# A graph layer's weights in 15 block products, with weight sums made by copies and accumulating transfers

## The chip, the cores and the metric

The kernel runs on one core of one Trainium2 chip. The metric is the device time of one execution in microseconds (us); the kernel before took 729.84 us, the median of three runs (729.0 to 730.84). Engines are named as in the profile: PE is the matrix engine, PEld its weight loads, DVE the vector engine, ACT the scalar engine, POOL the GpSimd engine, SP the engine that issues most transfers. All data are float32. One matrix multiply of the program appears in the profile as two, so 72 multiplies are counted as 144; such a half is called a piece below.

## The reference, cut to what matters

The program is an attention layer over a graph of 384 nodes, then a network of two relational graph layers. Only the second of these two layers is at issue (and the hand-over to it from the first). `l` counts the layers:

```python
x = relu(h_text @ w_in + b_in)                       # 384 x 768
for l in range(2):
    h_in = x
    W = einsum('rb,bio->rio', comp[l], basis[l])     # 4 bases, 6 relations, 768 x 768
    agg = ...                                        # sum over edges, mean per relation and node
    x = relu(agg + x @ root[l] + conv_bias[l]) + h_in
    x = bn_gamma[l] * (x - mean) * rsqrt(var + 1e-5) + bn_beta[l]   # over the nodes
h_final = x @ w_out + b_out
```

The kernel makes the products of x with the four bases and with the root, five products of [384, 768] by [768, 768] in each layer. The edges' part is applied to the four base products as one more matrix product, with a matrix `At` (four times 384 x 384) mixed from the six relations.

## The kernel before

The features lie turned, as `XT` (six chunks of 128 features on the partitions, 384 nodes along the row). A layer runs in this order.

For each base `b` in turn, nodes 0 to 255 and the two halves of features and outputs are taken as a 2 by 2 by 2 block product in seven products, and nodes 128 wide of the third block plainly. The multiplies are recorded at L985 (plain ones) and L979 (those with sums). Each has 384 columns. The weight sums are DVE work (`weight_sums`, L927 and L929; `last_sums`, L935), the feature sums too (`node_sums`, L920). ACT copies results out of PSUM into `H_` (L991 to L1006), and DVE adds others to them (L992, L1000, L1002). Weights come as three transfers a base through the ring of five buffers `wpool`.

Then comes the root, 36 multiplies of 384 columns (L1019) into six PSUM banks. In the first layer the mixes of `At` for that layer follow from L348 on; in the second they are dealt out between the products by the table `between` (L953 to L957): 20 DVE instructions (L348) and four of ACT (L346).

Last come the products of `H_` with `At`, in three pairs of output chunks, each by seven products of six multiplies of 192 columns (L1077). In a pair `p` the program's order is: product `pc` with the first sum; DVE takes it into `XN` (`take`, L1107); DVE normalises the chunk before (`normalise_layer`, L1054 to L1058); product `pa`; `take`; product into `pc` again; `take`; then ReLU on ACT (`rectify`, L1110), adding the old features and the node statistics on DVE with a square root on ACT (`measure`, L1042 to L1049). A bank that is multiplied into again must first have been taken by DVE.

The order on PE, DVE, ACT, POOL and SP is the program's own: each engine works through its instructions as written, and one that waits holds up all that stand behind it on that engine. POOL issues accumulating transfers elsewhere in the kernel: at L852 it adds the second count table in DRAM to `A` in SBUF.

Of the kernel before, what the change touches and what calls it, by code (L numbers as in the profile page):

```python
# [10 lines left out]
F32 = mybir.dt.float32  # L11
# [6 lines left out]
P = 128  # L18
N = 384
# [8 lines left out]
KC = DC // P  # L28
HC = DC // 2
HN = N // 2  # L30
R = 6
# [12 lines left out]


BQ, BK, BV, BIQ, BIK, BIV, B_IN, CB, GAM, BET, NCOL = 0, 8, 16, 24, 32, 40, 48, 54, 66, 78, 90

# [4 lines left out]
def gnn_kernel(ctx: ExitStack, tc: tile.TileContext, out, x, edges, chunks, cols, rows, small,  # L52
               wq, wk, wv, wiq, wik, wiv, wo, w_in, basis, root, w_out):
    nc = tc.nc
# [15 lines left out]
    def next_bank(name, among=range(8)):  # L70

        i = next(i for i in ring if i in among)
        ring.remove(i)
        ring.append(i)
        return bank(i, name)
# [13 lines left out]
    def wload(src, shape, name, whole=False):  # L89
        w = wpool.tile([P, *shape], F32, tag="w", name=name)  # L90
        load_rows(w, src, whole)
        return w
# [279 lines left out]
    with ExitStack() as inner:  # L372
# [358 lines left out]
        for g in range(STEPS + 1):  # L731
            f = g + LEAD
            if g < STEPS:
                turn_probs(g)
            if f < STEPS:
                exponents(f)
            if f - 1 in total:
                normalise(f - 1)
            if f + 1 < STEPS:
                scores(f + 1)  # L740
            if g == STEPS:
                ps_y = next_bank("ps_y", (0,))
                multiply_o(ps_y, 2, 0, range(KD - 1))
            if g > 0:
                gather(g - 1)
            if f + 2 == STEPS:

                w_x = [act_tile("w_x") for _ in range(2)]
                for half in range(2):
                    load_rows(w_x[half], w_in[half])  # L750
                w_first = [wload(basis[0, 0, part], (2, DC), "w_c") for part in range(3)]
                w_first += [wload(basis[0, 1, part], (2, DC), "w_c") for part in range(2)]
        soft_stack.close()
# [152 lines left out]
    with tc.tile_pool(name="conv", bufs=1) as cp:  # L906
# [4 lines left out]
        def block(X, n, i):  # L911

            return X.rearrange("p (c i) n -> p i c n", i=2)[:, i, :, n * P:(n + 1) * P]

        def node_sums(X):
            S = cp.tile([P, 4, 3, P], F32, tag="S", name="S")
            for i, a, b, op in ((0, block(X, 1, 0), block(X, 1, 1), ALU.add), (1, S[:, 0], block(X, 0, 0), ALU.subtract),
                                (2, block(X, 0, 0), block(X, 1, 0), ALU.subtract),
                                (3, block(X, 0, 1), S[:, 1], ALU.subtract)):
                nc.vector.tensor_tensor(S[:, i], a, b, op)  # L920
            return S

        def weight_sums(w):
            T13 = keep.tile([P, 3, 2, HC], F32, tag="hT", name="T13")
            T2 = keep.tile([P, 3, HC], F32, tag="mask8", name="T2")
            for c in range(3):
                nc.vector.tensor_tensor(T13[:, c], w[c][:, :, HC:], w[c][:, 0, :].rearrange("p (o d) -> p o d", o=2),  # L927
                                        ALU.subtract)
                nc.vector.tensor_tensor(T2[:, c], w[c][:, 1, HC:], T13[:, c, 0], ALU.subtract)  # L929
            return T13[:, :, 0], T2, T13[:, :, 1]  # L930

        def last_sums(w, T2):
            T4 = cp.tile([P, 3, HC], F32, tag="T4", name="T4")
            for c in range(3):
                nc.vector.tensor_tensor(T4[:, c], w[c][:, 1, :HC], T2[:, c], ALU.subtract)  # L935
            return T4
# [3 lines left out]
        def load_basis(l, b):  # L940
            w = w_first.pop(0) if w_first else []
            return w + [wload(basis[l, b, part], (2, DC), "w_c") for part in range(len(w), 3)]

# [4 lines left out]
        def mixes(l, r, *bs):  # L948
            return lambda: mix(l, r, At, bs)
# [3 lines left out]
                   (0, 3, 0): shares(4), (0, 3, 1): shares(5),  # L953
                   (0, 3, 4): lambda: [mix(0, r, At) for r in range(1, R)],
                   (1, 0, 0): mixes(1, 0, 0, 1, 2, 3)}
        for i in range(10):
            between[1, (i + 1) // 3, (i + 1) % 3] = mixes(1, 1 + i // 2, *((0, 1), (2, 3))[i % 2])  # L957

# [6 lines left out]
        for l in range(L):  # L965

            H_ = cp.tile([P, B, NT, DC], F32, tag="H", name="H")
            rest = lambda: None
            for b in range(B):
                hs = [[H_[:, b, n, i * HC:(i + 1) * HC] for i in range(2)] for n in range(NT)]  # L970
# [21 lines left out]
                nc.vector.tensor_tensor(hs[0][0], hs[0][0], pb, ALU.add)  # L992
                times(pc, S[:, 0], lambda c: T[0][:, c], True)
                nc.scalar.copy(hs[2][0], pe)
                nc.scalar.copy(hs[2][1], pf)
                nc.scalar.copy(hs[1][1], pc)
                times(pa, S[:, 1], lambda c: T[1][:, c])
                nc.scalar.copy(hs[0][1], pa)
                times(pc, S[:, 3], lambda c: w[c][:, 1, HC:])
                nc.vector.tensor_tensor(hs[0][1], hs[0][1], pc, ALU.add)  # L1000
                times(pa, S[:, 2], lambda c: T[2][:, c])
                nc.vector.tensor_tensor(hs[1][1], hs[1][1], pa, ALU.add)  # L1002
# [10 lines left out]

            w = [wload(root[l, part], (2, DC), "w_c") for part in range(3)]
            XN = xtp.tile([P, KC, N], F32, tag="XT", name="XN")
            pr = [next_bank("ps_c", [i for i in range(8) if i not in kept])[:, :N] for _ in range(KC)]
            for k in range(KC):
                for o in range(KC):
                    nc.tensor.matmul(pr[o], w[k // 2][:, k % 2, o * P:(o + 1) * P], XT[:, k, :], start=(k == 0),  # L1019
                                     stop=(k == KC - 1))  # L1020
                if k == 0:
                    rest()
                go_between(l, B, k)
            room2 = keep.tile([P, KD * N], F32, tag="hT", name="room2")
            spaces = [room2[:, 2304:]]
            if l + 1 < L:
                spaces += [v.rearrange("p i k o -> p (i k o)")[:, i * 768:(i + 1) * 768] for v, n in
                           ((cp.tile([P, 4, 3, P], F32, tag="S", name="sums"), 2),
                            (wpool.tile([P, 2, 6, P], F32, tag="w", name="sums"), 2)) for i in range(n)]
                spaces.append(cp.tile([P, 3, HC], F32, tag="T4", name="sums").rearrange("p c d -> p (c d)")[:, :768])  # L1030
                w = load_basis(l + 1, 0)
            else:

                room = late.tile([P, R * NT * N], F32, tag="A", name="room")
                spaces += [room[:, 3 * D + i * 768:3 * D + (i + 1) * 768] for i in range(5)]
                rowsB = room[:, :3 * D].rearrange("p (j d) -> p j d", j=3)
                for j, r in enumerate((R_BOUT, R_LNG, R_LNB)):
                    nc.scalar.dma_start(rowsB[:, j, :], rows[r:r + 1, :].to_broadcast([P, D]))

            def measure(o):  # L1040
# [38 lines left out]

            T1, T2 = [room2[:, i * 1152:(i + 1) * 1152].rearrange("p (c d) -> p c d", c=6) for i in range(2)]  # L1080
            T4 = keep.tile([P, 6, HN], F32, tag="mask8", name="T4")
            nc.vector.tensor_tensor(T1, q(0, 1), q(0, 0), ALU.subtract)
# [26 lines left out]
            def rectify(o):  # L1109
                nc.scalar.activation(XN[:, o, :], XN[:, o, :], AF.Relu)  # L1110
                return o
# [6 lines left out]
            pa = first_of(0)  # L1118
            for p in range(pairs):
                times(pr[2 * p][:, :HN], h(2 * p, 1), q(1, 0))  # L1120
            for o in range(KC):
                begin(o)
            take(0, 0, pa)
            ready = None
            for p in range(pairs):
                last = p == pairs - 1
                sums = iter(()) if last else feature_sums(p + 1)
                o0, o1 = 2 * p, 2 * p + 1
# [34 lines left out]
            XT = XN  # L1163
            if l + 1 < L:
                S = node_sums(XT)
                T = weight_sums(w)


        for t in range(NT):
            nc.gpsimd.tensor_tensor(x_sb[:, t, :], x_sb[:, t, :], rowsB[:, 2, :], ALU.add)  # L1170
        w = [wload(w_out[part], (2, D), "w_out") for part in range(3)]
        hf_ = cp.tile([P, NT, D], F32, tag="H", name="hf")
# [97 lines left out]
```

## Time and profile before

| What | Value |
|---|---|
| median of the runs | 729.84 us |
| the profiled execution's own time | 717.47 us |
| its span, first to last instruction | 715.7 us |
| first layer: last pair's products with `At` | 516.72 to 526.6 us |
| second layer: bases and root | 527.7 to 636.3 us |
| second layer: products with `At` | 636.3 to 677.3 us |
| last matrix product and layer norm | 677.3 to 715.7 us |

The profile numbers instructions by engine, line and shape. A group line gives how often it ran, the us in which it kept its engine busy and the mean ns of one. Matrix pieces overlap: one of 384 columns is listed at 486 ns, yet the next starts about 322 ns later; what counts for time is the distance between starts. A chain line gives a start, a length and what ran. A timeline line is alike, with the idle time before it in brackets.

### The profile page before, as it was taken

Reading aid. Unit: us, or ns where it says so; the run is one execution under the profiler, and the core shown is the slowest. Engines: PE = TensorE matmul, PEld = TensorE weight load, DVE = VectorE, ACT = ScalarE, POOL = GpSimd, SP = SyncE. Lnnn points to the kernel's source line nnn. Section 1 sums busy time; section 2 is a strip of 40 time slices with the busy share of each in tenths; the row PEclk is TensorE's granted clock in tenths of the full one; section 3 lists DMA queues with packets and bytes.
Section 4 is the critical chain, followed back from the end, with each engine's and each line's share of the span. In section 5 each row is a group of like instructions: output and inputs, shape, how many; then the busy total and the mean of one; then the engine's idle time right before and its main releaser. Section 6 shows DMA issues by size and latency. Waiting matters only on the chain.

```text
span 715.7 us, 9149 instructions
## 1 busy us (share of the span) xinstructions
PE 699.9 (98%) x3228; PEld 527.9 (74%) x3228; DVE 512.6 (72%) x1307; ACT 157.6 (22%) x360; POOL 308.1 (43%) x239
## 2 busy tenths in 40 slices
PE   8999999999999999999999999999999999999995
PEld 7759999999997444478985555558975555579943
DVE  5886697868886699787534279798878766507756
ACT  3211111111111577410221124202131111011100
POOL 1366777778687788687786542000000000120000
PEclk9999999999999999999999999999999999999999
DMA  8788787373562622733424994311104322700001
GB/s 303 267 279 264 228 250 212 80 243 67 203 209 43 177 2 1 221 44 45 89 0 103 250 288 153 133 44 45 45 0 133 102 69 94 308 1 1 1 30 59
DMA packets 69180, 91.04 MB, mean 127 GB/s; under 512 B 22940, under 2 KB 50688, under 8 KB 68750
## 3 DMA queue, kind: packets, MB, share of 16 engines
q1 hardware_dynamic: 46830, 78.45, 32.6%
q0 software_dynamic: 21296, 9.60, 10.8%
q10 hardware_dynamic: 1008, 2.41, 0.9%
q8 instruction: 25, 0.41, 0.2%
q14 instruction: 21, 0.17, 0.1%
HBM read 79.27 MB, written 11.16 MB: 126 GB/s over the span
## 4 chain that ended last, share of the span: by engine, by line
PE 87%; DVE 10%; ACT 2%; DMA 1%; issue 0%; DVEq 0%; ACTq 0%
PE ps_g L985 12%; PE ps_g L979 10%; PE ps_k L402 10%; PE ps_c L1077 10%; PE ps_v L402 8%; PE ps_q L420 6%; PE ps_q L402 5%; PE ps_f L1183 4%; DVE At L348 4%; PE ps_y L402 3%; PE ps_c L1019 3%; PE ps_x L402 3%; PE ps_o L707 2%; PE ps_s L662 2%; PE ps_pT L696 2%; PE ps_v L586 2%
## 5 line engine op out<-in xcount | busy, mean ns | idle before, releaser
L283 POOL DMA_INDIRECT atab<-count,at x99 | 166.3, 1679 | 44.2 <-issue 23.5
L278 POOL DMA_INDIRECT mtab<-m_val,at x99 | 103.4, 1045 | 57.6 <-issue 22.9
L1170 POOL TENSOR_TENSOR x_sb<-x_sb,room 128x1024 f32<-128x1024 f32 x3 | 7.0, 2348 | 188.9 <-DMA room<-in_rows 188.9
L348 DVE SCALAR_TENSOR_TENSOR At<-A,small_sb,At 128x1152 f32<-128x1152 f32 x40 | 53.6, 1414 | 0.0
L979 PE MATMUL ps_g<-T,S 128*128 128x384 f32 x144 | 49.1, 486 | 0.0
L985 PE MATMUL ps_g<-w_c,XN 128*128 128x384 f32 x144 | 47.7, 487 | 1.1 <-DVE XN L1107 1.1
L985 PE MATMUL ps_g<-w_c,XT 128*128 128x384 f32 x144 | 47.9, 486 | 0.0
L420 PE MATMUL ps_q<-hT,w_q 128*128 128x384 f32 (+1 forms) x160 | 43.4, 435 | 1.4 <-DVE hT L108 1.4
L985 PEld LDWEIGHTS ps_g<-w_c,XN 128*128 128x128 f32 x144 | 27.3, 190 | 20.2 <-DVE XN L1107 1.4
L979 PEld LDWEIGHTS ps_g<-T,S 128*128 128x128 f32 x144 | 27.3, 190 | 19.2 <-ACT H L991 0.4
L985 PEld LDWEIGHTS ps_g<-w_c,XT 128*128 128x128 f32 x144 | 27.3, 190 | 18.8
L420 PEld LDWEIGHTS ps_q<-hT,w_q 128*128 128x128 f32 x160 | 30.1, 200 | 14.1 <-ACT hT L101 1.7
L1077 PE MATMUL ps_c<-At,H 128*128 128x192 f32 x216 | 36.4, 326 | 0.0
L1077 PEld LDWEIGHTS ps_c<-At,H 128*128 128x128 f32 x216 | 35.4, 190 | 0.5
L402 PE MATMUL ps_k<-T,S 128*128 128x192 f32 x192 | 35.1, 326 | 0.0
L1107 DVE TENSOR_TENSOR XN<-XN,ps_c 128x192 f32<-128x192 f32 x38 | 12.5, 349 | 30.8 <-ACT XN L1063 19.7
L402 PEld LDWEIGHTS ps_k<-T,S 128*128 128x128 f32 x192 | 31.8, 190 | 0.0
L1183 PE MATMUL ps_f<-w_out,XN 128*128 128x512 f32 (+1 forms) x84 | 31.1, 531 | 0.0
L675 DVE CUSTOM_DVE_ANT_0 s<-ps_s,mask 128x384 f32<-128x384 f32 x48 | 24.5, 550 | 5.3 <-PE ps_s L662 5.3
L267 DVE SCALAR_TENSOR_TENSOR same<-cells,own,later 128x128 f32<-128x128 int32 x99 | 28.0, 350 | 0.4
L267 DVE SCALAR_TENSOR_TENSOR same<-keys,key,weigh 128x128 f32<-128x128 int32 x99 | 27.9, 349 | 0.0
L1183 PEld LDWEIGHTS ps_f<-w_out,XN 128*128 128x128 f32 x84 | 15.9, 190 | 14.9 <-issue 14.3
(298 smaller groups left out, 1411.6 us busy)
## 6 DMA issues: line engine op xcount, KB each, us to landing
w_c<-in_basis SPq DMA_DIRECT2D x96, 192.0 KB, 4.1
atab<-zero SPq DMA_DIRECT2D x36, 192.0 KB, 5.2
A<-atab POOLq DMA_DIRECT2D x12, 576.0 KB, 9.0
keys<-keys_d SPq DMA_DIRECT2D x25, 192.0 KB, 5.1
w_c<-in_root SPq DMA_DIRECT2D x6, 768.0 KB, 7.1
w_q<-in_wiq SPq DMA_DIRECT2D x16, 256.0 KB, 6.4
w_k<-in_wk SPq DMA_DIRECT2D x16, 256.0 KB, 5.8
w_k<-in_wik SPq DMA_DIRECT2D x16, 256.0 KB, 3.0
```

The lines of the kernel that those rows point to most:

```text
L267: nc.vector.scalar_tensor_tensor(same, row[:, n, :], mine[:, c:c + 1], times, ALU.is_equal, ALU.mult, accum_out=count[:, i, c:c + 1])
L278: nc.gpsimd.indirect_dma_start(mtab[c // PER][:, :], bass.IndirectOffsetOnAxis(at[:, 0, c:c + 1], 0), m_val[:, c:c + 1], None)
L283: nc.gpsimd.indirect_dma_start(atab[0 if i < 11 else i % 2][:, :], bass.IndirectOffsetOnAxis(at[:, 1, c:c + 1], 0), count[:, 1, c:c + 1], ...
L348: nc.vector.scalar_tensor_tensor(At[:, b], A[:, r], w, At[:, b], ALU.mult, ALU.add)
L402: nc.tensor.matmul(ps, a[:, k, :], b[:, k, :], start=start and k == 0, stop=(k == 3), skip_group_check=not start)
L420: nc.tensor.matmul(ps[o][:, c], wt_[:, k, o * P:(o + 1) * P], src[:, k, c], start=(k == 0 and c.start == 0), stop=(k == KD - 1 and c.stop ...
L675: nc.vector.tensor_tensor_reduce(s[j], ps[:, :N], mask8[:, t, :], -scale, 3.0e38, ALU.add, ALU.min, tops[:, j:j + 1])
L979: nc.tensor.matmul(ps, x[:, c], y(c), start=start and c == 0, stop=(c == 2), skip_group_check=not start)
L985: nc.tensor.matmul(ps, block(XT, n, i)[:, c], w[c][:, i, o * HC:(o + 1) * HC], start=(first and c == 0), stop=(c == 2 and (i == 1 or ps is ...
L1019: nc.tensor.matmul(pr[o], w[k // 2][:, k % 2, o * P:(o + 1) * P], XT[:, k, :], start=(k == 0), stop=(k == KC - 1))
L1077: nc.tensor.matmul(ps, x[:, c], y[:, c], start=start and c == 0, stop=stop and c == 5, skip_group_check=True)
L1183: nc.tensor.matmul(p, XT[:, k, t * P:(t + 1) * P], w[k // 2][:, k % 2, c0:c1], start=(k == 0), stop=(k == KC - 1))
```

## The change

The second layer's five products are no longer made by 2 by 2 by 2 blocks and a plain root. A new routine, `layer_by_15`, takes the features as 3 blocks of nodes by 2 of inputs and the weights as 2 blocks of inputs by 3 of outputs, and makes each product from 15 block products. The group numbers are g = 1 to 4 for the bases and g = 5 for the root. Products of the bases have 256 columns (three multiplies each), those of the root 128 (six each). Four PSUM chains a group are read while they grow.

The feature sums (`X_SUMS`, eleven) are made by DVE, one more by ACT. The weight sums (`W_SUMS`, ten a group, 128 x 768 each) are divided: five are DVE instructions; for the other five ACT copies one operand, with its sign, and a transfer from DRAM issued by POOL adds the other to it. The sixth field is the step at which a sum is put in the order, counted within its group, so that steps below 0 stand in the group before. For g = 1 the first four (W6, W13, W10 by copies and transfers, then W7 = W1 + W6 by DVE) are put at the head of the first layer's last pair (`p == 2`). Results leave PSUM 19 times a group: nine copies by ACT, ten additions by DVE. The root's result goes into `XN` this way, so ACT no longer begins it from PSUM (`begin`); the bias moves into `rectify`. The mixes go to steps 8, 11, 14 and so on.

The first layer keeps its products. Its root weights are loaded by outputs in place of by inputs, and the sums take their room from new tiles (`x_room`, `w_room`, `mroom`, `room2`).

```diff
+W_SUMS = (
+    (6, 1, 2, 1, 5, -7, True),
+    (13, -1, 2, 1, 0, -5, True),
+    (10, 1, 2, 1, 1, -3, True),
+    (7, 1, 1, 1, 6, -1, False),
+    (8, 1, 4, 1, 7, 0, False),
+    (9, 1, 0, -1, 6, 1, False),
+    (11, 1, 9, 1, 3, 2, True),
+    (12, 1, 4, 1, 11, 6, False),
+    (15, 1, 12, 1, 1, 7, True),
+    (14, 1, 12, -1, 13, 9, False),
+)
+PRODUCTS = (
+    (2, 1, 0, ((4, 1),)),
+    (6, 6, 1, ((7, 1), (8, -1))),
...
+    (3, 4, 3, ((4, 1),)),
+    (11, 5, 0, ((5, -1),)),
+    (12, 12, 3, ((3, -1),)),
...
+        def sum_weights(g, i):
+            dst, sa, a, sb, b, step, moved = W_SUMS[i]
...
+            if not moved:
+                signed_sum(w_places[place], sa, w_block(g, a), sb, w_block(g, b))
+                return
+            if sa > 0:
+                nc.scalar.copy(w_places[place], w_block(g, a))
+            else:
+                nc.scalar.activation(w_places[place], w_block(g, a), AF.Identity, scale=-1.0)
+            nc.gpsimd.dma_start(w_places[place].rearrange("p c o -> p (c o)").rearrange("p (n s) -> p n s", n=2),
+                                conv_w[g, b % 3, b // 3 * 2:b // 3 * 2 + 2].rearrange("n p s -> p n s"),
+                                accum_op=ALU.add)
...
+            for step in range(NPROD * (B + 1)):
+                g, k = 1 + step // NPROD, step % NPROD
+                while x_todo and x_todo[0][0] <= step + 3:
+                    sum_features(x_todo.pop(0)[1])
...
+                while w_todo and w_todo[0][0] <= NPROD + step:
+                    _, *what = w_todo.pop(0)
+                    sum_weights(*what)
...
+                if g <= B:
+                    for j in range(3):
+                        nc.tensor.matmul(ps, x[:, j], w[:, j], start=start and j == 0, stop=(j == 2),
+                                         skip_group_check=not start)
...
+                for to, sign in targets:
...
+                    if (g, to) in begun:
+                        nc.vector.tensor_tensor(dst, dst, src, ALU.add if sign > 0 else ALU.subtract)
+                    elif sign > 0:
+                        nc.scalar.copy(dst, src)
+                    else:
+                        nc.scalar.activation(dst, src, AF.Identity, scale=-1.0)
...
+                for behind, ahead, t in ((7, 1, 0), (10, 2, 2), (14, 2, 1)):
+                    if k == behind and g + ahead <= 10 - B:
+                        load_part(g + ahead, (2, 1, 0).index(t) if g + ahead == 10 - B else t)
...
+        sites = {}
+        for b in range(B):
+            sites[1 + 2 * b] = [mixes(1, 0, b)]
+        for i in range((R - 1) * B):
+            sites.setdefault(8 + 3 * i, []).append(mixes(1, 1 + i // B, i % B))
...
             for p in range(pairs):
                 last = p == pairs - 1
+                if last and l + 1 < L:
+                    free_from[:] = [999 if i in (1, 5) else 0 for i in range(len(w_places))]
+                    for i in range(4):
+                        sum_weights(1, i)
+                    free_from[1] = free_from[5] = 0
                 sums = iter(()) if last else feature_sums(p + 1)
                 o0, o1 = 2 * p, 2 * p + 1
                 pc = next_bank("ps_c")[:, :HN]
                 times(pc, S[p][0], T1, True)
                 take(o1, 1, pc)
```

## The prediction

> **What bounds the kernel now.** I read the page's busy shares, then the stage from base products to root by windows, then the chain.
>
> ```profile
> PE 699.9 (98%) x3228; PEld 527.9 (74%) x3228; DVE 512.6 (72%) x1307; ACT 157.6 (22%) x360; POOL 308.1 (43%) x239
> 527.70:636.30 108.60, 108.59 (x337) 64.08 (x338) 69.35 (x89) 16.80 (x30) 6.96 (x3) 1.00 0.32 116
> 527.71 11.88 PE ps_g L985 x36
> 616.99 19.35 PE ps_c L1019 x60
> ```
>
> PE is the bound. In the stage that changes (second line: stretch, length, then busy us of PE, PEld, DVE, ACT, POOL, then clock, DMA share, GB/s) PE has no gap at all; 336 pieces of 384 columns at 19.35 / 60 = 0.3225 us make 108.4. Fewer columns save time there as long as nothing else keeps PE waiting. DVE is busy for 69.35 us of it.
>
> The hand-over from the first layer is where the new sums enter. The timelines of DVE, ACT and PE:
>
> ```profile
> 519.38 0.15 DVE L1048 TENSOR_SCALAR sc<-mvb 128x1 f32<-128x1 f32 x1
> 519.45 0.34 DVE L1107 TENSOR_TENSOR XN<-XN,ps_c 128x192 f32<-128x192 f32 x1
> 519.57 0.20 ACT L1049 ACTIVATE sc<-sc 128x1 f32<-128x1 f32 x1 [1.63 <-DVE sc L1048]
> 518.67 2.11 PE L1077 MATMUL ps_c<-room,sums 128*128 128x192 f32 x12
> 520.62 2.11 PE L1077 MATMUL ps_c<-At,sums 128*128 128x192 f32 x12
> 527.71 1.24 PE L985 MATMUL ps_g<-w_c,XN 128*128 128x384 f32 x3 [1.07 <-DVE XN L1107]
> 530.92 0.48 DVE L1058 TENSOR_SCALAR XN<-XN,sc 128x384 f32<-128x384 f32 x1
> ```
>
> At 519.45 DVE takes bank `pc`; at 520.62 PE multiplies into `pc` again. Only 0.8 us lie between. The second layer's first product starts at 527.71, before the last chunk is normalised (530.92 + 0.48 = 531.40), since it reads early chunks.
>
> New kinds of work are priced from these (groups by form, timelines, and one line's page):
>
> ```profile
> L346 ACT ACTIVATE At<-A,small_sb 128x1152 f32<-128x1152 f32 x6 | 7.1, 1242 | 0.0
> L927 DVE TENSOR_TENSOR T<-w_c 128x768 f32<-128x768 f32 x12 | 11.4, 952 | 0.0
> L1187 DVE TENSOR_TENSOR hf<-ps_f,room 128x256 f32<-128x256 f32 x2 | 0.8, 424 | 2.8 <-PE ps_f L1183 2.8
> 322.80 3.62 PE L402 MATMUL ps_y<-hspace,A 128*128 128x256 f32 x16
> 17.16 1.04 PE L176 MATMUL ps_h<-ident,xn 128*128 128x128 f32 x8
> L143 PE MATMUL ps_warm<-ones x24: 274/275/371, 5.7 to 8.4; 128*128 128x128 f32 x24
> L852 POOL DMA_DIRECT2D A<-atab x6: 1290/1306/1316, 392.5 to 424.2; - x6
> DMA to landing us min/median/max: 7.3/9.0/10.3
> 12.90:17.10 4.20, 4.20 (x16) 4.20 (x17) 0.00 (x0) 0.00 (x0) 0.00 (x0) 0.62 0.98 376
> ```
>
> The L852 rows are the only accumulating transfers: 576 KB each, 7.3 us at best. The new ones have the same rows of 1536 bytes but 384 KB. Scaled by size: 4.9 / 6.0 / 6.9 us. The last line is PE after a pause (idle or transposing since 8.47): its clock averaged 0.62.
>
> **What the Trainium skill says.** *DMA: Bandwidth & Descriptors*, "Anatomy of one DMA — SWDGE (gpsimd) path", gives about 2.0 us plus bytes over 436 GB/s: 2.9 us for 384 KB. It would give 3.4 for 576 KB, where this trace shows 7.3 or more; the trace decides, and 2.9 is my lower end. *GPSIMD Engine Reference*, "1. Specifications", says that POOL's SBUF interfaces are shared with DVE, with contention when DVE reads two SBUF inputs. That fits, without proof, the quickest L852 transfer being issued at 407.44, with DVE busy for 0.5 of the next 2.7 us. *TensorE: Matmul & The Clock Gate*, "Part 1: The HAM clock gate", says that an idle window of about 3.4 us halves PE's clock until about as much busy time has passed; the 0.62 above agrees.
>
> **The change part by part.**
>
> *Products.* 256 columns: (3.62 - 0.38) / 15 = 0.216 us apart. 128 columns: (1.04 - 0.27) / 7 = 0.110 apart for transposes, (8.4 - 5.7) / 23 = 0.117 for the warm-up's multiplies, the first of which was still slow; I take 0.112. New PE work is 4 x 15 x 6 x 0.216 = 77.6 plus 15 x 12 x 0.112 = 20.1, together 97.7. Against 108.6 (527.7 to 636.3) that is **-10.9 us**. Were weight loads the limit at 128 columns (0.1625, the distance of 192-column pieces), the root would cost 9 us more; the warm-up pieces, each with its own load, speak against it.
>
> *Hand-over, W7.* At the head of the last pair the program puts three ACT copies with their transfers, then W7 on DVE, before `take` of `pc`. ACT reaches W6's copy only after the square root at 519.57. So: 519.8, copy 0.86 (768/1152 of L346, rounded up) to 520.7, POOL, landing 4.9 to 6 us later, 5.4 taken since DVE is idle then: 526.1. W7 0.95: 527.1. The `take` that stood at 519.45 ends at 527.5. PE, which wanted the bank at 520.62, stands **6.9 us**, beyond the 3.4 that lower its clock: about 1.6 us more. Product ends 531.1 instead of 522.6, and the rest of the tail (take, ReLU, statistics, twice) is unchanged: last chunk ready at 531.4 + 8.5 = 539.9. Behind the waiting DVE instruction stand six takes and three normalisations, and every later bank of PE's waits for one of them.
>
> *Second layer's start.* Product 0 needs early chunks, product 1 the sum x6, which DVE makes after the last normalisation: 539.9 + 0.55 = 540.45. Product 0 (1.29) fits before, so the layer runs as if begun at 539.15, against 527.71: **+11.4 us**. The whole hand-over thus eats the saving.
>
> *Inside the groups.* DVE per group: 5 sums x 0.95, 10 additions x 0.42, 5 mixes x 1.41 = 16.0 us of PE's 19.4. ACT: five copies and nine evacuations, 7.5 us. By busy time neither binds. But a loop runs through ordered queues: W11 = ACT copy 0.86, transfer A; W12 on DVE 0.95; W15's copy 0.86; an evacuation 0.35; next W6's copy 0.86 and transfer A, which starts behind W15's (1.5); W7 0.95; addition 0.42; mix 1.41; W8 and W9 1.90; W11 again. Without A: 10.1, and 0.5 for ten hand-overs. With A = 5.8: 22.2 per group against 19.4, so 2.8 us lost a group; at 4.9 1.0, at 6.9 5.0. It shows at product 8, which needs W12 and the addition queued behind it. Behind ACT's copy of W12 (for W15) stands the evacuation of product 7, for which product 9 waits, 1.29 us after product 8: inside the same pause. POOL has nothing but these transfers until the end's additions. Even with quick transfers W12 stands behind the mix of step 5: product 5 ends at 7.74, its addition at 8.3, the mix at 9.7, W12 at 10.7, the addition behind it at 11.1, where product 8 was due at 10.3; with what ACT's late evacuations add, a floor of about 1 us a group. Five groups at A = 5.8: 4.6 x 2.8 = **+12.9**; the first has no mixes before step 8 but gets its W9 late, the last starts no new sums.
>
> *Loads.* 15 weight parts of four 192 KB transfers replace 15 of as many bytes; the 25 accumulating transfers bring 9.8 MB more over some 110 us, 90 GB/s on top of the 116 in the windows. On SP they stand in ring order ahead of the three output-weight loads, which keep the 41 us of L1077 as cover. Two parts are loaded as product 7 ends, beside W15's and W6's transfers; that is the upper end of A.
>
> *Nothing.* Making sums for the `At` products (9.2 us of DVE, formerly under the root) now follows the root, under 48 pieces x 0.1625 = 7.8 us that need none of them; the first sum needed comes after 5.4 + 0.95 = 6.4. Without that cover it would cost 6.4. Root loads by outputs need their third part 2.6 us after the first layer's root starts instead of 15 us; its buffer comes free about 3 us before the root, and DVE's mixes set that stage's end. Zero, at most 2.
>
> Sum: 11.4 - 10.9 + 12.9 = +13.4. Profiled time 717.47 becomes 730.9; the median lies 12.4 above the profiled time, so 729.84 becomes **743.2**.
>
> **Rivals.**
> 1. *Quick transfers* (A of 3 to 5): the hand-over costs 8.7 to 11, the groups lose 5 to 7: +3 to +7, 733 to 737. For it: the skill's 2.9. Against: nothing below 7.3 in the trace.
> 2. *Slow transfers* (A of 7 and more, contended): 5 us a group, pauses long enough to lower the clock: +22 to +32, 752 to 762. For it: L852's maximum 10.3.
> 3. *Faster*: W6 lands before DVE needs it, or nearly so. Then the start is +3.0 (product 1 still waits for x6: 531.4 + 0.55 - 1.29), groups -10.9 + 5: -3, 727. It decides where A falls below about 1.5 us (stall 3.1, no lowered clock: 6 - 10.9 + 5 = 0); against it is that its copy stands behind the same square root as everything.
> 4. *DVE becomes the bound*: 16.0 of 19.4 says no, unless waits count; then it is case 2.
>
> **How the numbers follow.** My forecast 55% (its own range 738 to 750), rival 1 20%, rival 2 17%, rival 3 6%, the rest something else. Leaving out rival 3 and the worst of rival 2 gives 733 to 757. About 0.3% (2.2 us) is what a measurement of this kernel tells from no change: faster 0.06, same 0.04, slower 0.90.
>
> **What would show it.** Right: W7 on DVE waiting about 6 us for a transfer, a PE gap of 7 us at 520.6 with a lower clock after it; W12 waiting on a transfer in each group, PE pausing at product 8; PE pieces 0.216 and 0.112 apart. Wrong: accumulating transfers landing within 3 us, or PE without gaps from 520 to 640.

## The result, and the profile after

The changed kernel takes 760.94 us (median of 4 runs, 757.77 to 762.56); the kernel before took 729.71 us beside it. The ratio is 1.042, with a 95% interval of 1.038 to 1.046: 31.2 us slower, where 13.4 had been forecast. Some executions of either kernel run at a lower clock and take longer; ratios and differences of time below leave them out, except for the 50 us that one expectation names.

The changed kernel's profile also falls 11.8 us behind that of the kernel before ahead of everything studied here: 11.0 of them stand at 227 us, in the attention, which the change leaves alone. Other profiles of it and of its edits fall behind there by anything from nothing to 32 us. The kernel before seems to have such pauses too, since its timed runs lie 12 us above its profiled one, but no trace of it shows them. So I compare stretches and not end times.

The page of the changed kernel, busy time first, and then windows over two stretches: products to root, and all that follows. The columns of a window are stretch, length, busy us of PE, PEld, DVE, ACT and POOL, clock, DMA share, GB/s.

```profile
PE 708.1 (93%) x3432; PEld 562.3 (74%) x3432; DVE 535.4 (70%) x1344; ACT 178.7 (24%) x401; POOL 343.2 (45%) x264
550.67:673.72 123.05, 106.47 (x536) 91.68 (x537) 72.49 (x107) 37.56 (x71) 26.51 (x22) 0.94 0.72 161
673.72:760.03 86.31, 74.51 (x336) 58.90 (x335) 61.33 (x133) 5.52 (x15) 8.62 (x3) 0.94 0.10 37
```

PE is busy for 106.47 of 123.05 us where it had no gap before, at a clock of 0.94 instead of 1.00, and the DMA engines for 0.72 of the time instead of 0.32. The stretch after the root takes 86.3 us; before it took 79.4 (636.3 to the end of the span, 715.7). The forecast had put zero there, at most 2 us.

The hand-over: the timelines of ACT, POOL, DVE and PE, the instructions that match those shown of the kernel before.

```profile
531.36 0.20 ACT L1220 ACTIVATE sc<-sc 128x1 f32<-128x1 f32 x1 [1.63 <-DVE sc L1219]
531.47 0.81 ACT L1045 COPY w_room<-w_c 128x768 f32<-128x768 f32 x1
532.58 1.21 POOL L1048 DMA_DIRECT2D w_room<-in_conv_w  x1 [91.40 <-ACT w_room L1045]
537.58 0.96 DVE L1017 TENSOR_TENSOR room<-w_c,w_room 128x768 f32<-128x768 f32 x1 [6.25 <-DMA w_room<-in_conv_w]
538.45 0.35 DVE L1278 TENSOR_TENSOR XN<-XN,ps_c 128x192 f32<-128x192 f32 x1
538.85 3.88 PE L1248 MATMUL ps_c<-At,x_room 128*128 128x192 f32 x12 [6.26 <-DVE XN L1278]
551.30 0.55 DVE L1017 TENSOR_TENSOR x_room<-XN 128x384 f32<-128x384 f32 x1
551.96 2.38 PE L1086 MATMUL ps_g<-w_room,x_room 128*128 128x256 f32 x6 [4.04 <-issue]
```

W7 on DVE stands 6.25 us for W6's transfer, which ends 5.0 us after its issue; the take for bank `pc` comes behind W7, PE pauses 6.26 us, and its next twelve pieces take 3.88 us instead of 2.11. Product 1 starts as x6 is ready. From the square root at 531.36 to the start that product 1 amounts to (551.96 - 1.29 = 550.67) are 19.3 us; before, from 519.57 to 527.71, 8.1.

The same timelines around product 13 of the fourth group, which needs W15. L1045 is the copy of W12 into W15's place, L1048 its accumulating transfer (and W6's of the next group).

```profile
635.74 1.75 SPq L135 DMA_DIRECT2D w_c<-in_conv_w  x4
636.11 0.83 ACT L1045 COPY room<-mroom 128x768 f32<-128x768 f32 x1 [3.90 <-DVE mroom L1017]
637.25 2.43 POOL L1048 DMA_DIRECT2D room<-in_conv_w  x2 [6.00 <-ACT H L1105]
637.59 15.37 SPq L137 DMA_DIRECT2D w_out<-in_w_out  x2
648.11 2.90 PE L1086 MATMUL ps_g<-room,x_room 128*128 128x256 f32 x6 [4.91 <-DMA room<-in_conv_w]
```

The transfer issued at 637.25 lets product 13 begin at 648.11, 10.9 us later; loads of weights were issued beside it at 635.7 and 637.6. PE pauses 4.91 us, and its next six pieces then take 2.90 us instead of 1.46. A group's product 13 starts late by 2.1, 1.7, 2.4 and 5.1 us in groups 1 to 4, product 8 by 0.6 to 1.7.

After the root, DVE's sums (L1268) and POOL's additions (L1349):

```profile
679.29 0.95 DVE L1268 TENSOR_TENSOR x_room<-H 128x768 f32<-128x768 f32 x1
680.86 8.62 POOL L1349 TENSOR_TENSOR x_sb<-x_sb,room 128x1024 f32<-128x1024 f32 x3 [15.14 <-DMA room<-in_rows]
681.15 3.12 DVE L1268 TENSOR_TENSOR H<-H 128x768 f32<-128x768 f32 x1
684.19 3.09 DVE L1268 TENSOR_TENSOR x_room<-H,room 128x768 f32<-128x768 f32 x1
687.20 1.59 DVE L1278 TENSOR_TENSOR XN<-XN,ps_c 128x192 f32<-128x192 f32 x5
687.60 4.21 PE L1248 MATMUL ps_c<-x_room,room 128*128 128x192 f32 x12 [4.13 <-DVE XN L1278]
```

While POOL adds, sums of 128x768 take 3.1 us instead of 0.95. In the kernel before, the same three additions ran at 624.2 under the root, when DVE had no sums to make (its last one ended at 621.2):

```profile
624.22 6.96 POOL L1170 TENSOR_TENSOR x_sb<-x_sb,room 128x1024 f32<-128x1024 f32 x3 [188.85 <-DMA room<-in_rows]
```

### The profile page after: what moved, and what is told of

Same layout as the page of the kernel before. It is cut to its first block, busy times and chain, and to the rows that moved or that the text cites. A ratio compares the mean times of both kernels' runs of the same rounds, so it can differ in the third digit from the quotient of the medians.

```text
span 760.0 us, 9795 instructions
## 1 busy us (share of the span) xinstructions
PE 708.1 (93%) x3432; PEld 562.3 (74%) x3432; DVE 535.4 (70%) x1344; ACT 178.7 (24%) x401; POOL 343.2 (45%) x264
## 4 chain that ended last, share of the span: by engine, by line
PE 64%; issue 17%; DMA 10%; DVE 6%; POOL 1%; ACT 1%; DVEq 0%; POOLq 0%; ACTq 0%
PE ps_k L452 10%; PE ps_v L452 8%; PE ps_q L470 6%; PE ps_q L452 5%; PE ps_c L1248 5%; DMA A<-atab 5%; PE ps_g L1086 5%; PE ps_f L1362 4%; PE ps_y L452 3%; DMA room<-in_conv_w 3%; PE ps_s L712 3%; PE ps_x L452 3%; PE ps_o L757 2%; PE ps_pT L746 2%; PE ps_g L1091 2%
## 5 line engine op out<-in xcount | busy, mean ns | idle before, releaser
L328 POOL DMA_INDIRECT mtab<-m_val,at x99 | 106.8, 1079 | 55.4 <-issue 27.0
L1048 POOL DMA_DIRECT2D w_room<-in_conv_w x5 | 6.0, 1200 | 116.4 <-ACT w_room L1045 112.8
L1086 PE MATMUL ps_g<-room,x_room 128*128 128x256 f32 x144 | 38.2, 411 | 10.9 <-DMA room<-in_conv_w 7.1
L1048 POOL DMA_DIRECT2D room<-in_conv_w x16 | 20.0, 1338 | 61.9 <-ACT room L1045 36.8
L1086 PEld LDWEIGHTS ps_g<-room,x_room 128*128 128x128 f32 x144 | 29.3, 207 | 17.2 <-issue 7.1
L452 PE MATMUL ps_k<-T,S 128*128 128x192 f32 x192 | 36.7, 336 | 4.0 <-issue 2.0
L452 PEld LDWEIGHTS ps_k<-T,S 128*128 128x128 f32 x192 | 32.6, 195 | 4.9 <-issue 2.6
L1101 DVE TENSOR_TENSOR H<-H,ps_g 128x256 f32<-128x256 f32 x40 | 16.0, 417 | 23.8 <-PE ps_g L1086 13.7
L1196 PE MATMUL ps_c<-XT,w_c 128*128 128x384 f32 x72 | 23.5, 486 | 0.0
```

What stands on the lines that cost most here:

```text
L328: nc.gpsimd.indirect_dma_start(mtab[c // PER][:, :], bass.IndirectOffsetOnAxis(at[:, 0, c:c + 1], 0), m_val[:, c:c + 1], None)
L452: nc.tensor.matmul(ps, a[:, k, :], b[:, k, :], start=start and k == 0, stop=(k == 3), skip_group_check=not start)
L1048: nc.gpsimd.dma_start(w_places[place].rearrange("p c o -> p (c o)").rearrange("p (n s) -> p n s", n=2), conv_w[g, b % 3, b // 3 * 2:b // 3 ...
L1086: nc.tensor.matmul(ps, x[:, j], w[:, j], start=start and j == 0, stop=(j == 2), skip_group_check=not start)
```

## The experiments

All are edits of the changed kernel. "Hand-over" is the time from the square root of the last chunk of the second pair to product 1, less 1.29; "products" from there to the end of the second layer's root; "end" is the rest. Ratios are to the kernel before on the same chip; the chip differs between rows. The three profiles of the changed kernel itself (changed, after_again, after_third) differ by 3.9 us in "products", so a difference of that size between two rows shows nothing by itself; where less is read, it is from single pauses.

| run | ratio (95%) | hand-over | products | end |
|---|---|---|---|---|
| before | 1 | 8.1 | 108.6 | 79.4 |
| changed | 1.042 (1.038 to 1.046) | 19.3 | 123.1 | 86.3 |
| late_w7 | 1.030 (1.027 to 1.033) | 11.1 | 121.2 | 86.8 |
| no_transfers | 1.013 (1.011 to 1.016) | 12.4 | 106.3 | 88.1 |
| rows_by_dma | 1.034 (1.030 to 1.038) | 20.2 | 124.2 | 79.6 |
| no_part_loads | 1.030 (1.027 to 1.034) | 20.0 | 109.8 | 87.7 |
| loads_held | 1.053 (1.041 to 1.066) | 19.7 | 122.0 | 85.4 |
| w15_dve_again | 1.029 (1.021 to 1.036) | 19.8 | 110.9 | 88.4 |
| w15_mix_later | 1.030 (1.023 to 1.037) | 19.9 | 107.6 | 88.4 |
| two_by_dve | 1.033 (1.025 to 1.041) | 19.8 | 106.2 | 87.6 |
| best1 | 1.034 (1.024 to 1.044) | 6.9 | 122.6 | 79.4 |
| best2 | 1.004 (1.001 to 1.007) | – | – | – |
| best3 | 0.9935 (0.9911 to 0.9959) | 6.9 | 107.4 | 79.9 |
| after_again | 1.064 (1.052 to 1.077) | 19.8 | 119.1 | 85.4 |
| after_third | – | 19.6 | 122.6 | 86.6 |

**W7 out of the last pair (late_w7).**

```diff
-                    for i in range(4):
+                    for i in range(3):
                         sum_weights(1, i)
```

> Edit: W7 is left out of the last pair of the first layer and made with the second layer's first sums. Theory (DVE's queue stands in W7 behind W6's transfer): the PE pause of 6.3 us at bank pc goes, the second layer begins about 3.5 us late instead of 11.2, and W7, now behind the sums x6 to x8, costs products 1 and 2 about a microsecond: 8 us less than the changed kernel, 753 (range 751 to 756). Rival (the pause is only moved, since products 1 to 3 now wait for W7 and W8): at most 3 us less, 758 to 761.

738.64 us against 716.10: 22.5 over, where the changed kernel had 31.2. PE's timeline at the hand-over:

```profile
518.95 2.11 PE L1248 MATMUL ps_c<-At,x_room 128*128 128x192 f32 x12
522.85 2.11 PE L1248 MATMUL ps_c<-At,H 128*128 128x192 f32 x12
524.80 1.46 PE L1086 MATMUL ps_g<-w_c,XN 128*128 128x256 f32 x6
```

No pause is left in these products, and twelve pieces take 2.11 us each time. The hand-over is 8.2 us shorter; 3.0 stay, the wait of product 1 for x6. The theory holds in place and size.

**No transfers (no_transfers).** ACT's copies stay, the transfers behind them go; 25 sums then lack their second block.

```diff
-            nc.gpsimd.dma_start(w_places[place].rearrange(...), conv_w[...], accum_op=ALU.add)
```

> Edit: the accumulating transfers of the moved weight sums are left out, the ScalarE copies stay (so 25 of the weight sums lack their second block). Theory (the transfers' time is what the groups and the hand-over lose): hand-over 8 us less, the groups' loss of 25 us falls to the floor of about 5 that the order on DVE and ACT leaves: about 27 less, 733.5 (range 730 to 738). Rival (DVE's and ACT's queues themselves hold PE up): only the hand-over's 8 and a few more, 747 to 753.

10.0 us over the kernel before: 21 less, not 27. Products fall by 16.8 us to 106.3, which is 8.6 above the bare 97.7. This is the floor that the order on DVE and ACT leaves: in groups 2 to 4 it is 1.3 us each (0.7 of it ahead of product 8), but 3.7 in the first, where the sums of features and weights come all at once. The transfers are the larger part of the loss; the floor had been set too low.

**The rows without POOL's additions (rows_by_dma).**

```diff
-        for t in range(NT):
-            nc.gpsimd.tensor_tensor(x_sb[:, t, :], x_sb[:, t, :], rowsB[:, 2, :], ALU.add)
...
+                for t in range(NT):
+                    nc.gpsimd.dma_start(x_sb[:, t, :], rows[R_LNB:R_LNB + 1, :].to_broadcast([P, D]), accum_op=ALU.add)
                 for g, t in ((1, 2), (1, 1), (1, 0), (2, 2), (2, 1)):
```

> Edit: the three POOL additions to x_sb near the end become three accumulating transfers of the same row, issued behind the first layer's root. Theory (POOL's additions slow DVE's sums threefold after the second root): the sums 128x768 take 0.95 us again, the pause of 4.1 us goes: 7 us less than the changed kernel, 754 (range 752 to 756). Rival (the pause is that the sums now stand behind the root without cover): 0 to 2 us less, 759 to 761.

DVE and PE after the root, now from 665.5:

```profile
672.96 0.95 DVE L1270 TENSOR_TENSOR H<-H 128x768 f32<-128x768 f32 x1
673.83 0.95 DVE L1270 TENSOR_TENSOR x_room<-H,room 128x768 f32<-128x768 f32 x1
674.70 1.60 DVE L1280 TENSOR_TENSOR XN<-XN,ps_c 128x192 f32<-128x192 f32 x5
675.11 2.21 PE L1250 MATMUL ps_c<-x_room,room 128*128 128x192 f32 x12
```

The sums take 0.95 us again, PE has no pause, and the end is 79.6 us: 6.7 less, and what it was before. In the whole time it was 5.4 less (25.8 over). That the sums now follow the root costs nothing; that POOL's additions meet them does.

**Fewer part loads (no_part_loads).** Groups 2 to 5 multiply the first group's blocks. (The trace counts 48 transfers less than before this edit, 12 parts and not 14.)

```diff
-            parts[g, t] = wload(conv_w[g, t], (KC, HC2), "w_c") if g < 10 - B else ...
+            parts[g, t] = parts[1, t] if 1 < g < 10 - B else wload(conv_w[g, t], (KC, HC2), "w_c") if g < 10 - B else ...
```

> Edit: groups 2 to 5 of the second layer use the first group's blocks in their products, so that 14 loads of weight parts are left out; all sums and transfers stay. Theory (the part loads delay the accumulating transfers that are issued beside them): W15's transfer lands 5 to 6 us after its issue instead of 7.3 to 10.7, the groups lose 12 us less: 749 (range 745 to 753). Rival (the transfers delay each other on their own queue): W15 and W6 stay at 7 us and more, 757 to 761.

The landing times of accumulating transfers, from the page of their line, first in late_w7, which has the part loads, then without these. The profile shows the landing of only 18 of the 25 in late_w7 and of 6 in this run:

```profile
DMA to landing us min/median/max: 5.1/7.9/10.7
```

```profile
DMA to landing us min/median/max: 5.1/5.6/7.5
```

That product 13 waits at most 0.8 us in any group says the same of the transfers whose landing is not shown. The products take 13.3 us less (9.3 in the whole time). The same transfers on the same queue are quick without the loads, so queueing behind each other is not the cause; running beside the loads is. The trace of late_w7 agrees. These are windows from issue to landing of a quick transfer, away from the loads, and of a slow one beside them:

```profile
583.54:588.71 5.17, 5.17 (x26) 4.55 (x25) 3.08 (x4) 0.38 (x1) 1.19 (x1) 1.00 0.50 76
591.93:601.54 9.61, 7.06 (x33) 5.91 (x33) 3.53 (x7) 2.80 (x6) 3.85 (x4) 1.00 1.02 219
```

The DMA share is 0.50 for the quick one and 1.02 for the slow one. DVE was busy for 60% of the quick one's time and for 37% of the slow one's, so a busy DVE does not explain the delay. Compared with no_transfers, 3.5 us stay as the price of transfers left to themselves, which is less than two profiles of one kernel can differ.

**The loads held back (loads_held).**

```diff
+                if k == 11 and g <= B:
+                    nc.sync.dma_start(gate, dst[:1, :64])
-                for behind, ahead, t in ((7, 1, 0), (10, 2, 2), (14, 2, 1)):
+                for behind, ahead, t in ((11, 1, 0), (11, 2, 2), (14, 2, 1)):
```

> Edit: the two part loads that start as product 7 ends are held back until product 11 is evacuated, by a transfer of 256 bytes ahead of them on SP that reads its block; every sum, transfer and load stays. Theory (it is the meeting with the part loads that delays W15's and W6's transfers): they land after 5 to 6 us as in the run without these loads, the groups take 110 to 113 us instead of 123: 11 us less than the changed kernel (8 to 13). Rival (not when the loads run but how many bytes move in all): at most 4 us less.

Product 13 waits no more in any group, yet the products take 122.0 us. DVE and PE in the fourth group:

```profile
634.38 0.96 DVE L1017 TENSOR_TENSOR room<-w_c,room 128x768 f32<-128x768 f32 x1 [0.86 <-DMA w_c<-in_conv_w]
...
642.09 0.96 DVE L1017 TENSOR_TENSOR mroom<-w_c,room 128x768 f32<-128x768 f32 x1 [1.59 <-DMA room<-in_conv_w]
...
643.43 2.07 PE L1087 MATMUL ps_g<-mroom,x_room 128*128 128x256 f32 x6 [2.20 <-DVE H L1102]
```

W9 now waits for a part that was held back, so W11, made from it, is issued later, and W12 waits for W11; product 8 starts 2.0 to 3.6 us late instead of 0.6 to 1.7 (at most 2.2 in the other profiles of the changed kernel), and in four groups product 10 up to 1.3 us late as well. Neither theory is borne out as put. The rival's number fits (1.0 us less), but not its reason: when the loads run does decide whether W15 is late, and holding them only moved the pause to the next deadline. The whole time lies 11 us below the changed kernel's on the same chip, as the theory said, but by chance: its profile is 11.6 us ahead of that one already at the square root, before any of this.

**W15 by DVE (w15_dve, w15_dve_again).**

```diff
-    (15, 1, 12, 1, 1, 7, True),
+    (15, 1, 12, 1, 1, 7, False),
```

> Edit: W15 is summed by DVE, without copy and transfer; the other four moved sums stay. Theory (the pauses ahead of product 13 are W15's transfer, late behind the part loads): these pauses and the lowered clock after them, 16 us in the changed kernel's profile, go, and DVE's added 4.8 us give 1 to 3 back: 14 us less than the changed kernel (10 to 17). Rival (the pause only moves, to W12 behind W11's transfer or W7 behind W6's): 6 us less or not even that.

> Edit: as the run w15_dve, whose timed runs scattered too widely for a ratio: W15 alone is summed by DVE. Theory (product 13's pauses are W15's transfer): the layer's products take 109 to 112 us instead of the changed kernel's 123 and 119, its ratio to the kernel before falls from 1.042 to 1.025 (1.02 to 1.03). Rival (the pause moves to W12 or W7): 1.035 or more.

The first run gave no ratio. In the second, product 13 starts on time in all groups, products take 110.9 us, and the ratio is 1.029: the theory's, though with an interval up to 1.036. Product 8 keeps 1.1 to 1.7 us.

**Where product 8's pause comes from (w15_mix_later, two_by_dve).** The first moves the mixes, the second makes W11 by DVE too and leaves the mixes where they were.

```diff
-            sites.setdefault(8 + 3 * i, []).append(mixes(1, 1 + i // B, i % B))
+            sites.setdefault(9 + 3 * i, []).append(mixes(1, 1 + i // B, i % B))
```

> Edits: W15 summed by DVE, and every mix after the first four one product later, so that W12 stands ahead of the mix of its step instead of behind that of the step before. Theory (product 8's pause of 1 to 1.4 us a group is W12 behind a mix, as the floor was worked out): it falls below 0.3 us where W11's transfer lands in time, 4 us less than with W15 alone. Rival (W12 waits for W11's transfer, which takes 5 us wherever the mix stands): less than 1.5 us gained.

> Edit: W11 and W15 summed by DVE, nothing else, so that no sum of a group waits for a transfer of the same group. Theory (product 8's pause, left when W15 alone or the mixes are moved, is W11's transfer): product 8's pause falls to the 0.7 us that it has without any transfer, product 13's is gone, the products take 105 to 108 us. Rival (DVE, now with 17.9 of 19.4 us a group, is late with sums or additions): 110 or more.

DVE and PE around product 8 of the second group with the mixes moved, and then the window over the products and product 8 of the third group with both sums on DVE:

```profile
583.60 0.96 DVE L1017 TENSOR_TENSOR w_room<-w_c,room 128x768 f32<-128x768 f32 x1 [2.65 <-DMA room<-in_conv_w]
584.48 0.41 DVE L1101 TENSOR_TENSOR H<-H,ps_g 128x256 f32<-128x256 f32 x1
584.95 1.56 PE L1086 MATMUL ps_g<-w_room,x_room 128*128 128x256 f32 x6 [1.93 <-DVE H L1101]
```

```profile
549.99:656.14 106.15, 101.10 (x535) 88.07 (x536) 80.45 (x117) 29.81 (x61) 14.43 (x12) 0.98 0.58 149
604.77 1.56 PE L1086 MATMUL ps_g<-room,x_room 128*128 128x256 f32 x6 [0.52 <-DVE H L1101]
```

With the mixes moved W12 stands 2.65 us in W11's transfer, and product 8's pause stays at 0.9 to 2.1 us, as the rival said. Yet the products take 3.3 us less than with W15 alone, near the theory's 4: what goes is half a microsecond or more ahead of product 14 in each of the first four groups and 0.7 us ahead of product 3 in the last, pauses that neither had named. With W11 on DVE the delay of product 8 in groups 2 to 4 is 0.69 us, as without any transfer, and the products take 106.2 us. DVE is busy for 80.5 of them and holds nothing up. (By total time this run is not better than w15_dve_again, 1.033 beside 1.029, but the intervals overlap and are wider than the 4.7 us between their products.)

**Together (best1, best2, best3).** Besides the edits above, all three make W6 a pair earlier, and W7 to W9 and x6 (which reads only early chunks) in the last pair:

```diff
+                if p == 1 and l + 1 < L:
+                    sum_weights(1, 0)
...
+                    sum_weights(1, 3)
+                    nc.vector.tensor_tensor(x_sums[0], XN[:, :3, P:2 * P], XN[:, :3, 2 * P:], ALU.subtract)
                 take(o0, 1, pc)
```

> Edits together: the part loads held back as in the run of that name; W6 made a pair earlier, W7 to W9 and x6 made in DVE's pauses of the last pair; the mixes one product later, behind W12; the rows added by three transfers. Theory: products -10.9, hand-over +1 to +2, groups +4 (product 8 no longer waits), end 0: 5 us less than the kernel before, ratio 0.993 (0.986 to 1.002). Rival (sums in DVE's pauses delay the takes and the chain of normalisations, and the moved mixes delay additions): ratio 1.005 or more.

> Edits together: W15 summed by DVE; mixes one product later; W6 a pair earlier, W7 to W9 and x6 in DVE's pauses of the last pair; rows added by three transfers; part loads as in the changed kernel. Theory: products -10.9, hand-over +2, groups +4 to +5, end 0, together 5 us less than the kernel before, ratio 0.993 (0.988 to 1.000). Rival (W12 still waits for W11, and the loads for W7 to W9): groups +8 to +10, ratio 1.000 to 1.005.

> Edits: as best2, and W11 summed by DVE too, so that only W6, W13 and W10 of the next group are moved. Theory (DVE has 18 of 19.4 us a group and no wait on a transfer is left inside a group): groups +2 to +4, ratio 0.991 (0.985 to 0.998). Rival (DVE at 93% of a group is the bound, its additions and sums come late and PE pauses in every group): groups +8 or more, ratio 1.000 or more.

best1 holds the loads back and so keeps a pause in every group (products 122.6): its theory fell with that of loads_held. best2, with W15 on DVE in place of that, is 1.004, the rival's value (only its time is used here). best3, with W11 on DVE too, is 0.65% faster than the kernel before, clear of its interval: 723.5 us beside 727.9. Its three stretches add up to 194.2 us, where before they took 196.1. The products by windows:

```profile
528.15:635.50 107.35, 101.12 (x542) 89.77 (x542) 83.08 (x126) 30.75 (x64) 14.24 (x12) 0.98 0.59 150
```

Of the 9.7 us over the bare products, 3.3 are product 2, which waits for x7 behind the last normalisation, and 4.3 a pause in the fifth group at W10's transfer, with the lowered clock behind it. Its third group runs its 15 products in 19.43 us without a pause, where two_by_dve took 20.73. The mixes' place is the one difference between the two that reaches this group, so the 1.3 us a group that were left in no_transfers and two_by_dve come from there, as the forecast had said of product 8.

**The changed kernel again (after_again, after_third).**

> No edit: the changed kernel beside these variants on their chip. The first comparison gave 31.2 us over the kernel before, ratio 1.042. Theory (hand-over 11.2, groups 14.3, end 7.1 are causes of the second layer and nothing else): again 29 to 34 us over the kernel before, whatever that takes on this chip. Rival (part of it is from pauses earlier in the program, which differed between the two profiles): less than 25.

> No edit: the changed kernel again. Theory (its whole loss lies in the hand-over, the products and the stretch after the root, 11 + 14 + 7 us in the first profile): 27 to 34 us over the kernel before, and as much in these three stretches of the profile. Rival (the 50 us of the second comparison are real, and some 20 of them lie in code that the change leaves alone): 40 or more, with the last pair of the first layer beginning later than in the kernel before.

The totals missed their ranges: 47.6 us over the kernel before on one chip, and 34.7 on the other, just above the range. The three stretches hold better: over those of before they sum to 28.2 and 32.7 us (11.7 + 10.5 + 6.0, and 11.5 + 14.0 + 7.2), against 32.6 in the first profile (11.2 + 14.5 + 6.9). That explains all but 2 of the 34.7 us, and leaves 19 of the 47.6 open. Both profiles are late before the stretches begin: the square root stands at 529.0 and 551.4 instead of 519.6, and nearly all of that stands already at 227 us, in code the change leaves alone. What makes PE pause there was not studied.

## Why the prediction was wrong

*Direction and products: right.* The groups' own work is as priced: 15 products of 1.29 us; in two_by_dve groups 3 and 4 start 20.73 us apart, 19.4 of work and 1.3 of pauses. The weight loads at 128 columns do not limit the root.

*Hand-over, W7, and second layer's start: right.* +11.2 us measured, +11.4 forecast, through the wait, the pause, the lowered clock and the wait for x6 as named; late_w7 takes the transfer's part away. The landing was worked out as 5.4 us, and was 5.0. That size is in part luck: it was scaled down from transfers that ran beside loads, and taken because DVE is idle then, while a transfer of late_w7 landed in 5.17 us with DVE busy for 60% of them.

*Inside the groups: wrong, +25.4 us instead of +12.9.* The step that failed is the one value A = 5.8 us for the accumulating transfers of its loop, W11's and W6's. Transfers issued away from loads land after about 5 us, but W15's and those behind it run beside two part loads, and took up to 10.7 (late_w7). The forecast had these loads in view and took them for "the upper end of A", 6.9 us, where they set the usual value. It also looked for the pause in the wrong place: the loop puts it ahead of product 8, and W15's own transfer enters it only as 1.5 us of issuing ahead of W6's. But W15 has a deadline, product 13, five products (6.5 us) after its copy can start. Of the 25.4 us, 16.8 come from the transfers (no_transfers), 13.3 of which need the loads beside them (no_part_loads); by the changed kernel's quickest profile (products 119.1) these would be 12.8 and 9.3. The other 8.6 are the floor, forecast as about 5.

The trace of before could have shown it. Its accumulating transfers all ran beside 26 loads of `w_c` on SP (issued from 387.04 on, over 45 us). The four whose landing is shown took 7.3, 8.8, 9.2 and 10.3 us, at a DMA share of 0.80, 0.97, 1.13 and 1.11 from issue to landing, while DVE was busy for 50, 97, 31 and 63% of that time: the share comes close to ordering them, DVE does not. The quickest and the slowest by windows:

```profile
407.44:414.74 7.30, 7.30 (x24) 4.33 (x23) 3.67 (x6) 0.48 (x1) 6.13 (x6) 1.00 0.80 177
411.57:421.83 10.26, 10.26 (x33) 6.04 (x32) 6.46 (x11) 1.68 (x3) 5.45 (x6) 1.00 1.11 295
```

Scaling them by size did not hold either: where the DMA share was 0.97 and more, 384 KB took 7.7 to 10.7 us in late_w7, as long as these 576 KB.

The second rival, slow transfers with 5 us lost a group, comes nearest (25.4 / 5 = 5.1). But 1.7 of the 5.1 are the floor, and the measured time, which lies in its range, holds the 6.9 us at the end that it too had put at nothing.

*Nothing: wrong, +6.9 us at the end instead of 0.* The cover that the step named did hold: PE starts on the first sum at 681.36, as the 48 pieces end. What failed is that the step moved DVE's sums without asking what else runs then. The rows' load stands on ACT's queue behind the root's last evacuation (672.47; before it landed in time for additions at 624.2), so POOL's additions to `x_sb`, which the sum never priced, meet the sums. The forecast had read in *GPSIMD Engine Reference*, "1. Specifications", of the Trainium skill that the two engines contend for SBUF where DVE reads two SBUF inputs, and applied it to transfers; it bears on these additions, and the trace agrees (0.95 to 3.1 us), while the windows of late_w7 show none for transfers.

*The sum.* The groups were short by 12.5 us and the end by 6.9, the hand-over long by 0.2: 19.2 of profile, against a miss of 17.7 in the medians (760.9 for 743.2). Its price by *DMA: Bandwidth & Descriptors*, "Anatomy of one DMA — SWDGE (gpsimd) path", 2.9 us for 384 KB, was rightly left as the lower end: the quickest took about 5. The fourth rival, "DVE becomes the bound", is refuted by best3, where DVE is busy for 83 of 107 us and the products still run at their bare pace for a whole group.

## What to carry to other kernels

Price a transfer by what runs beside it where it is issued: set its issue against the loads that start with it and against the first consumer of its result, one deadline for each transfer, not one average for all. A transfer that was measured beside loads prices only transfers beside loads. A transfer that saves a microsecond of an engine with slack (here DVE, 83 of 107 us in the fastest version) is a loss as soon as one consumer waits for it. When work moves, list everything that moves with it in every queue, loads on other engines and the additions behind them too.

## What the runs showed of the hardware

- Beside POOL's TENSOR_TENSOR, DVE's sums of two SBUF blocks ran at a third of their speed (128x768: 3.1 us for 0.95), while DVE's additions with one operand in PSUM kept theirs (five of 128x192 in 1.59 us, 1.60 without POOL). POOL's three additions took 8.62 us, and 6.96 in the kernel before, where DVE made no sums beside them. The figures would fit two engines that take turns (one sum and one addition are 0.95 + 6.96 / 3 = 3.27 us), but no run tests that.
- An accumulating transfer of 384 KB landed in about 5 us at best. Of those whose landing is shown, the median was 5.6 us in the run without part loads (6 transfers, 7.5 at most), and 7.9 in late_w7 with them (18 transfers, 10.7 at most; 11.6 in rows_by_dma).
- PE's clock fell after shorter pauses than the 3.4 us that the forecast took as what lowers it: in the changed kernel after 1.97 and 2.19 us (the 4.3 us from 572.84 and from 620.85 ran at a mean clock of 0.61). In late_w7 it stayed at 1.00 after a pause of 2.55 us (599.44 to 603.00), so the length of the pause alone does not decide it.
